# Image tiles kept as sums and differences of neighbours along the width, with filters rewritten for them, and the column levels of three batches moved to VectorE

## The chip, the cores and the metric

The kernel runs on one core of one Trainium2 chip. The metric is the device time of one execution in microseconds (us); lower is better. The engines are called as in the profile: PE (TensorE, matmuls), PEld (its weight loads), DVE (VectorE), ACT (ScalarE), POOL (GpSimd) and SP (SyncE, which here only issues DMAs).

## The reference

The input is x of shape (4, 64, 256, 256): 4 batches, 64 channels, images of 256 by 256, all in float32. Four layers follow each other.

```
layers 0, 1, 3:  y = conv2d(x, outer(hx, hy)) + x * bias      per channel, causal in both axes
                 hx, hy: 256 taps a channel, from a small sine network times a decay
layer 2:         f1 = haar2d(x)                               full 2-D Haar transform
                 acc = sum over i in (0, 1) of
                       shrink(einsum('bchw,oc->bohw', f1 * v[i], conv_w[i]), tau[i])
                 y = haar2d(acc, inverse=True) + x            shrink(f, t) = sign(f) * relu(|f| - t)
```

The filter of a convolution is an outer product, so a convolution is one causal product along the rows of the image and one along its width. A step of the Haar transform takes sums and differences of neighbours.

## The kernel before, in words

**A convolution.** For each batch b and channel c the image lies in SBUF as a tile of 128 partitions by 2 by 256, where row k * 128 + p is at partition p. `toeplitz` loads a tile `t` of 128 by 2 by 256 with one DMA from a padded filter in DRAM (`pads`): partition p gets the filter shifted by p, first the row filter, then the width filter. `contract` (L253, L254) multiplies the image as stationary operand with the filter read backwards. Since the filter is causal, the second half of the image meets only 128 columns. Each such product leaves the image transposed, so a product along the rows (`first`, to `pa`, copied to SBUF as `a` by ACT in L267) and one along the width (`second`, to `py`) bring it back. DVE adds bias times the input (`residual`, L284).

**Conv stage.** `convolutions` runs layers 0 and 1 for a batch: load `x`, `a0`, `y0`, `a1`, `y1`. Then `pairs` (L329, L330) takes sums and differences of neighbours along the width, the first level of the Haar transform. Both go to DRAM (`keep`). `levels` makes the further levels along the width, two of them on DVE and five on POOL, four channels at a time (L342, L343). `split` and `rest` (L361, L366) cut the result into two fp32r parts, `down` (L373, to `pz`) transforms along the columns with two matmuls, `away` stores to `coef`.

**Mixing stage.** `mixing` takes 64 groups of coefficients: `mix` is the matmul over channels (L441, to `px`), the scaling by v is shared by DVE (L460) and ACT (L465), then size and sign on ACT (L469, L472), and shrink, sign and sum on DVE (L476, L480, L486). The result collects in the resident tile `z`.

**Inverse stage.** `inverse` turns `z` back into images. The levels along the columns are done in place on `z` by DVE (`level`, `halve`: L291, L292), for chunks 1 to 3 of 16 channels each. For chunk 0, the first 16 channels, they are done by a matmul instead: after `rows` (L533, L534, to `pw`), `halves` (L540 on ACT, L541 on DVE) splits in two fp32r parts, and `cols` (L547, to `pu`) multiplies. `join` (L555, L558, L559) adds half of `keep` and spreads sums and differences back to neighbours, giving `u`. Then comes the convolution of layer 3 and the output, whose DMA ACT issues. Every third channel of batches 0 to 2 is put off: its `u` goes to DRAM (`late`), and its last convolution runs beside the mixing stage of batch 3 (`convolution`).

**Order.** Every step is entered with a time in ticks (a channel's or a group's turn) plus an offset from the table `PLACE`. The steps are sorted by that time and written out. The tile framework then orders each engine's instructions by their dependencies, and each engine works in its own order. Batch b+1's conv stage runs beside batch b's mixing stage; the inverse stage of b follows. `BUFS` and the `bufs` arguments give the number of buffers of a tag; a tile waits until the buffer used that many tiles ago is free. `toep` has 6.

## Time and profile before

| what | us |
|---|---|
| median of 3 runs | 2877.34 (2877.28 to 2879.65) |
| profiled execution, its own time | 2875.0 |
| its span, first to last instruction | 2873.2 |

In the span the stages lie as follows (first to last instruction of L441 and L533, rounded): conv of batch 0 alone to 446; mixing 0 to 868; inverse 0 to 1062; mixing 1 to 1523; inverse 1 to 1711; mixing 2 to 2172; inverse 2 to 2356; mixing 3 to 2641; inverse 3 to the end.

Rows of the page name the line, the engine, the operation, the tiles as out<-in, the shape and the count; then busy time in us, the mean of one in ns, and the idle time of the engine before them with what ended it. "128x256" is 128 partitions by 256 elements. One float32 matmul of the program is two instructions of the profile.

### The profile page before, as it was taken

How to read it: one execution, taken by the hardware profiler on the slowest of the kernel's cores; microseconds unless marked ns; L12 is line 12 of the kernel's file. 1: busy time of each engine (PE TensorE's matmuls, PEld its weight loads, DVE VectorE, ACT ScalarE, POOL GpSimd, SP SyncE). 2: the span in 40 equal slices, each digit the busy share in tenths (PEclk: the TensorE clock that was granted, in tenths of full speed). 3: DMA queues.
4: the chain of work that ended last, by engine and by line, in shares of the span. 5: the costliest groups of instructions: out<-in, count | busy, mean ns of one | idle time of the engine just before them, and what ended most of it. 6: DMA issues, size and time to landing. Idle time of an engine off the chain costs nothing. (4 is left out here: it accounts for less than half of the span.)

```text
span 2873.2 us, 52387 instructions
## 1 busy us (share of the span) xinstructions
PE 2819.8 (98%) x16566; PEld 2550.2 (89%) x16566; DVE 2498.0 (87%) x4263; ACT 2080.4 (72%) x4950; POOL 339.4 (12%) x644
## 2 busy tenths in 40 slices
PE   8999999999999999999999999999999999999999
PEld 6899998888888898998898998998888998888998
DVE  4655558999999779999999779999999779999985
ACT  2333338999995558998995658999995659998554
POOL 0111111121121001221221001221121000000000
PEclk9999999999999999999999999999999999999999
DMA  5877777666676986777777986777777988787786
GB/s 162 260 231 231 230 234 223 208 211 205 202 213 214 291 251 197 215 213 214 209 207 235 299 257 195 216 213 213 212 208 233 299 265 235 230 238 213 224 241 200
DMA packets 599367, 649.77 MB, mean 226 GB/s; under 512 B 48465, under 2 KB 517044, under 8 KB 598964
## 3 DMA queue, kind: packets, MB, share of 16 engines
q1 hardware_dynamic: 536996, 578.61, 68.2%
q10 hardware_dynamic: 62096, 67.82, 6.7%
q8 instruction: 134, 2.20, 0.3%
q14 instruction: 141, 1.16, 0.1%
HBM read 426.77 MB, written 219.48 MB: 225 GB/s over the span
## 5 line engine op out<-in xcount | busy, mean ns | idle before, releaser
L253 PE MATMUL py<-t,a 128*128 128x256 f32 x3072 | 922.2, 382 | 9.9 <-ACT a L267 9.2
L267 ACT COPY a<-pa 128x512 f32<-128x512 f32 x768 | 478.9, 624 | 495.5 <-PE pa L254 453.4
L465 ACT ACTIVATE f<-px,vt 128x64 f32<-128x64 f32 x2816 | 610.6, 367 | 101.4 <-DVE f L460 101.0
L254 PEld LDWEIGHTS py<-t,a 128*128 128x128 f32 x3072 | 583.4, 190 | 79.3
L254 PE MATMUL py<-t,a 128*128 128x128 f32 x3072 | 590.0, 274 | 0.0
L253 PEld LDWEIGHTS py<-t,a 128*128 128x128 f32 x3072 | 497.3, 191 | 51.1 <-ACT a L267 19.3
L441 PE MATMUL px<-wb,f 128*128 128x256 f32 x2048 | 487.6, 380 | 7.4 <-ACT f L465 7.3
L441 PEld LDWEIGHTS px<-wb,f 128*128 128x128 f32 x2048 | 369.0, 190 | 49.8 <-ACT f L465 10.2
L343 POOL TENSOR_TENSOR sd<-less 128x128 f32<-128x128 f32 (+4 forms) x320 | 192.7, 602 | 1855.5 <-DVE less L342 1537.6
L526 ACT COPY zc<-z 128x512 f32<-128x512 f32 x256 | 281.9, 1104 | 108.4 <-PE pw L534 99.6
L476 DVE TENSOR_TENSOR mag<-mag,vt 128x1024 f32<-128x1024 f32 x256 | 316.6, 1237 | 12.2 <-ACT mag L469 11.3
L480 DVE SCALAR_TENSOR_TENSOR mag<-mag,f 128x1024 f32<-128x1024 f32 x256 | 316.5, 1238 | 0.0
L253 PE MATMUL pa<-t,y 128*128 128x256 f32 x1024 | 308.9, 383 | 6.7 <-DVE y L284 5.2
L253 PE MATMUL pa<-t,x 128*128 128x256 f32 x1024 | 305.7, 380 | 0.0
L469 ACT ACTIVATE mag<-f 128x1024 f32<-128x1024 f32 x256 | 295.7, 1155 | 2.7 <-DVE z L486 0.4
L366 DVE TENSOR_TENSOR sp<-sd,sp 128x512 fp32r<-128x512 f32 x256 | 179.8, 702 | 127.8 <-ACT sp L361 126.7
L472 ACT ACTIVATE f<-f 128x1024 f32<-128x1024 f32 x256 | 285.8, 1116 | 3.5
L253 PE MATMUL pa<-t,u 128*128 128x256 f32 x772 | 232.1, 382 | 6.5 <-ACT w L540 2.8
L284 DVE SCALAR_TENSOR_TENSOR y<-x,bsb,py 128x512 f32<-128x512 f32 x256 | 190.7, 745 | 42.1 <-PE py L254 41.8
L254 PEld LDWEIGHTS pa<-t,y 128*128 128x128 f32 x1024 | 194.5, 190 | 26.3
L254 PEld LDWEIGHTS pa<-t,x 128*128 128x128 f32 x1024 | 194.6, 190 | 26.3
L284 DVE SCALAR_TENSOR_TENSOR y<-y,bsb,py 128x512 f32<-128x512 f32 x256 | 190.6, 745 | 27.7 <-PE py L254 27.3
(72 smaller groups left out, 4406.6 us busy)
## 6 DMA issues: line engine op xcount, KB each, us to landing
t<-pad SPq DMA_DIRECT2D x768, 256.0 KB, 4.1
x<-in_x SPq DMA_DIRECT2D x256, 256.0 KB, 3.8
coef<-co SPq DMA_DIRECT2D x256, 256.0 KB, 3.2
f<-coef SPq DMA_DIRECT2D x256, 256.0 KB, 3.1
r<-keep SPq DMA_DIRECT2D x256, 256.0 KB, 4.1
out_y<-y ACTq DMA_DIRECT2D x193, 256.0 KB, 4.2
keep<-sums SPq DMA_DIRECT2D x256, 128.0 KB, 2.9
keep<-sd SPq DMA_DIRECT2D x256, 128.0 KB, 2.8
```

Of the source, the lines that this page charges most:

```text
L253: nc.tensor.matmul(ps[:, m, :], src[:, 0, m * P : (m + 1) * P], t[:, ::-1], start=True, stop=False)
L254: nc.tensor.matmul(ps[:, m, P:], src[:, 1, m * P : (m + 1) * P], t[:, : P - 1 : -1], start=False, stop=True)
L267: nc.scalar.copy(a, s["p" + new])
L284: nc.vector.scalar_tensor_tensor(y, s[res], bsb[:, layer, c : c + 1], s["p" + new], ALU.mult, ALU.add)
L343: engine.tensor_tensor(t[:, :, :, half:length], v[..., 0], v[..., 1], ALU.subtract)
L441: nc.tensor.matmul(ps[:, q, h, :], f[:, q, h * P : (h + 1) * P], wb.rearrange("p r n -> p (r n)"), start=True, stop=True,)
L465: nc.scalar.mul(f4[:, j], px[:, j], scale(g, 0)[:, j : j + 1])
L469: nc.scalar.activation(mag, st[g]["f4"], AF.Abs)
L472: nc.scalar.activation(st[g]["f4"], st[g]["f4"], AF.Sign)
L476: nc.vector.tensor_sub(mag, mag, over(g, 1, 16))
L480: nc.vector.scalar_tensor_tensor(mag, mag, 0.0, st[g]["f4"], ALU.max, ALU.mult)
L526: nc.scalar.copy(a.rearrange("p h k i -> p (h k) i"), z[:, c // 16, :, :, c % 16].rearrange("p i x -> p x i"))
```

## The change

**Layout.** An image tile is now 128 by 4 by 2 by 64: for each half of the rows and each half of the width first 64 sums, then 64 differences of neighbours. The input and the output arrays are handed over with neighbours apart (even columns, then odd columns), one row of 2 KB a partition. POOL turns the input into sums and differences (`pairs`, now ahead of the convolutions) and turns the output back (`neighbours`; the very last one on DVE), two additions of 256 elements each. The sum of y1 writes straight to `sums` and `sd`, and `join` straight to `u`.

**Filters.** The row filter stays. The width filter is written in the basis of sums and differences: `filters` makes four runs of it (`runs`), and `toeplitz` fills the second half of `t` from these with two DMAs of 64 partitions; a third loads the first half. `along_width` reads this half of `t` as h, e, n with both h and n backwards, in runs of 64.

**Column levels.** In batches 0 to 2 chunk 0 takes the same way as the others, through `level`; `halves` and `cols` stay for batch 3 only. Where the levels stand has changed: for these batches more of them stand in the mixing stage, and the later ones are cut into pieces of 8, some with an order that keeps them behind the joins.

**Buffers.** Images, inputs, `u` and outputs share the tag "y", now with 9 buffers.

The diff, cut to its core:

```diff
-BUFS = {"res": 1, "y": 5, "co": 3}
+BUFS = {"y": 9, "co": 3}
 PLACE:
-    "load": 0.714,
+    "load": -1.0,
+    "pairs": 0.1,
+    "bands": 0.714,
-    "pairs": 4.639,
-    "out": 4.537,
+    "neighbours": 3.543,
+    "out": 5.2,
-    "l out": 4.4,
+    "l neighbours": 3.48,
+    "l out": 4.8,
 filters, end():
-            for axis, queue in enumerate((nc.scalar, nc.sync)):
-                queue.dma_start(pads[layer][:, axis, :], f[axis * C : (axis + 1) * C])
+            nc.sync.dma_start(pads[layer], f[:C])
+            g0, g1, g2 = (f[C:, i : i + S : 2] for i in range(3))
...
+            nc.vector.tensor_add(sums, g0, g2)
+            nc.vector.tensor_sub(less, g0, g2)
+            nc.vector.scalar_tensor_tensor(w[:, 0, 0, :P], sums, 0.5, g1, ALU.mult, ALU.add)
+            nc.vector.tensor_scalar(w[:, 0, 1, :P], less, -0.5, None, ALU.mult)
+            nc.vector.tensor_scalar(w[:, 1, 0, :P], less, 0.5, None, ALU.mult)
+            nc.vector.scalar_tensor_tensor(w[:, 1, 1, :P], sums, -0.5, g1, ALU.mult, ALU.add)
+            nc.scalar.dma_start(runs[layer], w)
 toeplitz:
-        nc.sync.dma_start(t, ap(pads[layer], c * 2 * ROW, [[1, P], [ROW, 2], [1, S]]))
+        nc.sync.dma_start(t[:, 0], ap(pads[layer], c * ROW, [[1, P], [1, S]]))
+        for i in range(2):
+            nc.sync.dma_start(
+                t[i * H : (i + 1) * H, 1].rearrange("p (o n) -> p o n", o=2),
+                ap(runs[layer], (c * 2 + i) * 2 * RUN, [[1, H], [RUN, 2], [1, P]]),
+            )
+    def along_width(ps, src, t):
+        t = t.rearrange("p (e h n) -> p h e n", e=2, h=2)[:, ::-1, :, ::-1]
+        v = ps.rearrange("p k (h e n) -> p k h e n", h=2, e=2)
+        for k in range(2):
+            for m in range(2):
+                nc.tensor.matmul(
+                    v[:, k, 1] if m else v[:, k],
+                    src[:, m, k * P : (k + 1) * P],
+                    t[:, 0] if m else t,
+                    start=(m == 0),
+                    stop=(m == 1),
+                )
+    def butterflies(engine, t, name):
+        new = io.tile([P, 4, 2, H], F32, name=name, tag="y", bufs=BUFS["y"])
+        engine.tensor_add(new[:, :, 0], t[:, :, 0], t[:, :, 1])
+        engine.tensor_sub(new[:, :, 1], t[:, :, 0], t[:, :, 1])
+        return new
 residual, for y1:
+                for e, to in enumerate((sums[:, c % 4], sd[:, c % 8, 1])):
...
+                    nc.vector.scalar_tensor_tensor(to, s[res][:, :, e], scale, ps[:, :, e], ALU.mult, ALU.add)
 pairs:
-            nc.vector.tensor_add(sums[:, c % 4], v[:, :, :, 0], v[:, :, :, 1])
-            nc.vector.tensor_sub(sd[:, c % 8, 1], v[:, :, :, 0], v[:, :, :, 1])
+            st[c]["x"] = butterflies(nc.gpsimd, st[c]["x"], f"xb_{b}_{c}")
 join:
-            nc.vector.scalar_tensor_tensor(t, st[c]["r"], 0.5, ps, ALU.mult, ALU.add)
...
-            nc.vector.tensor_add(v[:, :, :, 0], t[:, 0], t[:, 1])
-            nc.vector.tensor_sub(v[:, :, :, 1], t[:, 0], t[:, 1])
+            for e in range(2):
+                behind[0] = nc.vector.scalar_tensor_tensor(u[:, :, e], r[:, e], 0.5, w[:, e], ALU.mult, ALU.add)
 inverse:
+        if b + 1 < B:
+            for chunk in range(4):
+                for n in (1, 2, 4, 8):
+                    when(along + 12 + 3 * chunk, n, chunk)
+                when(along + 20 + 3 * chunk, 16, chunk)
+            for chunk in range(2):
+                for i in range(2):
+                    when(along + 37 + i + 3 * chunk, 32, chunk, 16 * i, 16)
+                for i in range(3 - chunk):
+                    when(along + 43 + 8 * i + 3 * chunk, 64, chunk, 16 * i, 16)
...
-            if c < 16:
+            if c < 16 and b + 1 == B:
                 at(start + c + PLACE["halves"], halves, c)
                 at(start + c + PLACE["cols"], cols, c)
 last:
+        def neighbours(c):
+            engine = nc.vector if b + 1 == B and c + 1 == C else nc.gpsimd
+            st[c]["y3"] = butterflies(engine, st[c]["y3"], f"out_{b}_{c}")
```

## The prediction

> **What bounds it now.** I read the page's busy times first, then busy times by stage, then the costliest groups, then single instructions where two engines compete.
>
> ```profile
> PE 2819.8 (98%) x16566; PEld 2550.2 (89%) x16566; DVE 2498.0 (87%) x4263; ACT 2080.4 (72%) x4950; POOL 339.4 (12%) x644
> ```
>
> PE is busy 98% of the span, and the granted clock is 1.00 in every stage. But 87% for DVE is a mean over unlike stages. Here the span is cut by stage: mixing and inverse of batch 0, of batch 1, then (after batch 2, like batch 1) of batch 3.
>
> ```profile
> 446.00:868.00 422.00, 416.30 (x2310) 371.58 (x2309) 414.07 (x696) 389.62 (x1109) 83.27 (x134) 1.00 0.69 208
> 868.00:1062.00 194.00, 185.17 (x1204) 168.70 (x1203) 162.72 (x294) 111.68 (x146) 7.21 (x17) 1.00 0.84 260
> 1062.00:1523.00 461.00, 458.83 (x2584) 413.50 (x2583) 449.11 (x743) 403.27 (x1127) 89.88 (x140) 1.00 0.71 208
> 1523.00:1711.00 188.00, 185.79 (x1218) 171.03 (x1217) 150.55 (x289) 113.11 (x148) 7.60 (x20) 1.00 0.86 274
> 2356.00:2641.00 285.00, 276.06 (x1497) 246.47 (x1497) 280.89 (x413) 268.37 (x702) 0.00 (x0) 1.00 0.78 230
> 2641.00:2863.00 222.00, 220.45 (x1447) 204.16 (x1446) 185.23 (x317) 115.34 (x145) 0.00 (x0) 1.00 0.75 226
> ```
>
> After the stage's length come the busy times of PE, PEld, DVE, ACT and POOL. In the mixing stages PE and DVE are both full (458.8 and 449.1 of 461). In the inverse stages PE alone is. In mixing 3 DVE is the fuller one (280.9 of 285), and POOL does nothing. So the time moves by what PE loses, by what PE waits for, and by what happens to DVE in mixing.
>
> **The change, part by part.**
>
> *Matmuls of the column levels.* L540, L541 and L547 go for 48 channels, 16 in each of three inverses.
>
> ```profile
> L547 PE MATMUL pu<-w,hb 128*128 128x512 f32 x128 | 46.4, 439 | 0.0
> L541 DVE TENSOR_TENSOR w<-pw,w 128x512 fp32r<-128x512 f32 x64 | 43.6, 686 | 0.2 <-ACT w L540 0.2
> L329 DVE TENSOR_TENSOR sums<-y 128x256 f32<-128x256 f32 x256 | 108.8, 425 | 2.7
> L330 DVE TENSOR_TENSOR sd<-y 128x256 f32<-128x256 f32 x256 | 108.6, 424 | 0.0
> L555 DVE SCALAR_TENSOR_TENSOR t<-r,pw 128x512 f32<-128x512 f32 x192 | 131.7, 686 | 67.5 <-PE pw L534 58.8 <-DMA r<-keep 5.0
> L558 DVE TENSOR_TENSOR u<-t 128x256 f32<-128x256 f32 x256 | 108.8, 425 | 6.3
> ```
>
> The busy time would price a pair at 46.4/64 = 0.725 us, but matmuls overlap. In the conv-only stage the like pair of L373 sits between an L254 issued at 300.14 and the next L253 at 300.83; without a pair that step takes 0.22 (301.26 to 301.48). So a pair costs 0.47, and 48 cost 22.6 (at most 34.8 by the busy time). All of it is on the full engine: **-22.6**.
>
> *Convolution matmuls.* The order of instructions of both kernels has the same 6144, with the same columns. New is that the filter of the width product is read in runs of 64 where it was one reversed run of 256. No row shows PE reading broken runs. Near rows are DVE's L329, which reads every second element (425 ns against 423 of the contiguous L187), and ACT's L385, which writes in regrouped runs (660 against 624 of L267). DVE's says nothing; ACT's 5.8% on 768 products of 1.30 us would be +58. I take 0, because only the addresses change, as in DVE's row; a gain is excluded, since no column goes.
>
> *DVE, convolutions.* L329 and L330 go (0.85 us a channel). The sum of y1 (745 ns for 512 elements) becomes two of 256: between 0.42 (the 256-element rows) and 0.49 (plus the 59 ns by which L284 exceeds L555), so 0.92 for two. A channel saves 0.67; the 59 channels inside mixing 1 save 40.
>
> *DVE, levels.* Chunk 0 adds 2 x (0.22+0.29+0.42+0.69+1.23+2.45+4.90) = 20 us a batch at the rows of L291/L292. But the scheduler of before already pulled levels into mixing 1. Counting the program orders between first scaling and last add, level work there goes from 46 to 42 us, in mixing 0 from 32 to 42. Together DVE loses 44 us in mixing 1 and 2, and 53 x 0.67 - 10 = 26 in mixing 0; mixing 3 stays as it was.
>
> *DVE, inverses.* A join is two operations of 256 instead of 686 + 425 + 424 ns: 0.67 less for 64 channels, and 11 us of L541 go. PE's idle time there is 8.8, 2.2 and 2.8 us in inverses 0 to 2, most of it at the first channels, where the removed route and the levels queue on DVE. I take 8 of 13.8 back, and 3 of the 8.9 around mixing 3's end and the 1.6 of inverse 3: **-11**. In mixing 1 and 2, where DVE was as full as PE, PE gives up its 2.2 us of idle each and about as much in delayed issues: **-8**, between 0 and -10.
>
> *POOL.* New are 1022 additions of 256 elements: two for each input in conv (128 in each of mixing 0 to 2), two for each output (126 in mixing 3, 86 in an inverse). In the conv-only stage POOL takes 292 ns for 64 and 393 for 128 elements, so 0.6 us for 256, 1.2 a channel of 5.7 to 7 us: no bound by itself. The price is on DVE, and the rows show it:
>
> ```profile
> L342 POOL TENSOR_TENSOR less<-less 128x128 f32<-128x128 f32 x17 | 6.7, 393 | 0.0
> ```
>
> ```profile
> L342 POOL TENSOR_TENSOR less<-less 128x128 f32<-128x128 f32 x14 | 10.8, 775 | 1.8 <-DVE sd L343 1.8
> ```
>
> ```profile
> 1250.34 0.62 DVE L343 TENSOR_TENSOR sd<-less 128x256 f32<-128x256 f32 x1
> 1250.88 1.21 DVE L480 SCALAR_TENSOR_TENSOR mag<-mag,f 128x1024 f32<-128x1024 f32 x1
> 1252.02 1.42 DVE L476 TENSOR_TENSOR mag<-mag,vt 128x1024 f32<-128x1024 f32 x1
> 1253.36 0.73 DVE L284 SCALAR_TENSOR_TENSOR y<-x,bsb,py 128x512 f32<-128x512 f32 x1
> ```
>
> ```profile
> 1251.04 2.55 POOL L342 TENSOR_TENSOR less<-less 128x128 f32<-128x128 f32 x2 [0.36 <-DVE sd L343]
> 1253.54 0.29 POOL L343 TENSOR_TENSOR sd<-less 128x64 f32<-128x64 f32 x1
> ```
>
> The first row is POOL's in the conv-only stage, the second the same operation in mixing 1: 393 against 775 ns. Then one piece of mixing 1: two POOL operations of 0.69 together last 2.55 while DVE runs operations with two inputs in SBUF, and DVE's L476 (mean 1.23) takes 1.42, its L343 0.62 for 0.43. Once DVE runs the sum that reads PSUM, POOL goes at full speed. So one such cluster (ten POOL operations, 496 elements) cost DVE 0.38 us, or 0.20 scaled to 256 elements; the rise of DVE's means over the stage comes to some 0.21 a cluster, or 0.11. I take **0.15 an addition**, with 0 and 0.6 as ends: 19 us a mixing stage. In mixing 0 to 2 that is less than the 26 and 44 that DVE loses: 0. In mixing 3 nothing covers it: 19 less DVE's slack of 4, **+15** (-0 to +72).
>
> The Trainium skill, page "SBUF — State Buffer", section "Who interferes with whom", says that a DVE instruction with two SBUF inputs and a GpSimd instruction that reads SBUF exclude each other for the whole instruction. Taken at its hardest, each addition would hold DVE for its whole 0.6 us, which is the upper end above; the rows show POOL doing most of the waiting.
>
> *DMA and SP.* A filter tile comes in three DMAs, not one: 1536 more issues at 0.36 to 0.44 us, 1.6 us a channel in conv. SP waits 169 of 300 us between 100 and 400, and the additions take 85 of it. Bytes stay; rows of 512 B against 1 KB for half the filter, 2 KB against 1 KB for inputs and outputs. Each DMA waits for the one eight issues before it: ten a channel, all at today's slowest landing there (4.3 us), need 5.4 of the 5.67 us. 0, with little margin. ACT's output DMA now waits for POOL, 1.66 ticks (4.8 us) after it could start: 0.
>
> *Ends.* Six small operations behind each filter (1.5 us) lie under the warming matmuls: +1 (0 to 3). The last output gets two additions on DVE: **+0.9**.
>
> Sum: -22.6 - 11 - 8 + 15 + 1 + 0.9 = -24.7. The profiled execution took 2875.0 (span 2873.2 and 1.8 around it), the median 2877.3. So 2850 against the profiled one, 2852 as a median.
>
> **Rivals.**
> *Contention on DVE decides (slower).* With d us lost per addition, mixing 3 loses 126d - 4, mixing 0 128d - 26, mixing 1 and 2 128d - 44 each. The other terms give -39.7; from d = 0.28 on the change is a loss. At 0.43 (a 256-element operation of DVE's length) it is 50+29+11+11-40 = +61, 2938; at 0.6 about +148, 3025. For it: DVE is full in mixing, two thirds of its time has two SBUF inputs. Against: 0.11 to 0.20 measured. Chance 0.18.
> *PE reads broken runs slower.* +58 on the forecast, 2910. Chance 0.04.
> *SP or the eight in flight become the bound in conv.* From 4.6 us a landing on; at 5.0 the tick is 6.25, 64 x 0.58 = +37 in the conv-only stage alone, 2889. Chance 0.05.
> *The work leaves PE, but the joints hide it:* waits at stage borders stay and mixing 3 takes the rest, 2872 to 2883 or just under. Chance 0.09.
> *No contention and all waits go:* -22.6 - 25 - 10 + 2 = -56, 2821. Chance 0.09.
>
> **Numbers.** Forecast 2852, 0.55 (d from 0 to 0.26, 2833 to 2871). A measurement here tells 0.2% (5.8 us). Faster: 0.55, the last rival's 0.09 and half of the hidden case, 0.68. Same: the rest of that case and 0.05 of contention and SP near their deciding points, 0.10. Slower: 0.22. The range 2815 to 2895 takes in d up to 0.34 and SP's price, and leaves out the hard contention and broken runs.
>
> **What would show it.** L547's successor with 32 instead of 128 matmuls; PE about 2790 busy; DVE near 2180 and what POOL costs it, POOL at 1000 to 1700 with means far over 0.6 us in mixing; mixing 1 within 10 us of its length, mixing 3 longer by 10 to 20, inverses 0 to 2 shorter by 8 to 18. Wrong if DVE's 1024-element means in mixing rise by over 0.1 us, if PE's 256-column step leaves 0.22 us, or if PE waits for filter DMAs.

## The result, and the profile after

The changed kernel takes 3072.9 us (median of 4 runs, 3068.1 to 3080.4) against 2877.3 us of the kernel before: 1.0678 times as long, with an interval of 1.0665 to 1.0692. It is slower by 196 us where 25 us less was forecast. The profiled execution took 3072.6 us, its span 3070.8. The busy times of the whole span, from the page of the changed kernel:

```profile
PE 2873.0 (94%) x16470; PEld 2547.3 (83%) x16470; DVE 2417.7 (79%) x3882; ACT 2053.5 (67%) x4902; POOL 1304.9 (42%) x1666
```

PE was busy 98% of the span before and is 94% now; DVE 87% and 79%. POOL went from 339 to 1305 us. No engine but POOL is fuller than it was, and yet the span is 198 us longer: the time went into waiting. The stages show where. From here on the span is cut by one rule, the matmuls to `px`: "conv" runs to the first of a batch, "mixing" from its first to its last, "inverse" on to the next batch's first. (The prediction's cut gave the mixing stages of before some 14 to 26 us more and the inverses as much less.) The columns are those of the prediction's table; the rows are inverse 0, mixing 1, mixing 3 and inverse 3 of the changed kernel.

```profile
909.00:1135.00 226.00, 208.39 (x1298) 185.35 (x1297) 147.22 (x276) 115.93 (x158) 87.21 (x118) 0.99 0.82 243
1135.00:1596.00 461.00, 440.38 (x2430) 390.81 (x2429) 429.85 (x656) 387.25 (x1095) 219.22 (x250) 1.00 0.71 198
2509.00:2820.00 311.00, 278.55 (x1432) 236.29 (x1431) 305.49 (x387) 257.75 (x677) 136.36 (x115) 0.99 0.73 205
2820.00:3071.00 251.00, 239.40 (x1546) 220.87 (x1545) 169.34 (x284) 126.82 (x172) 121.62 (x142) 0.99 0.77 214
```

Mixing 1 and mixing 3 of the kernel before, by the same cut:

```profile
1063.00:1497.00 434.00, 431.83 (x2423) 388.89 (x2422) 422.42 (x704) 385.42 (x1091) 85.34 (x131) 1.00 0.71 208
2356.00:2627.00 271.00, 264.70 (x1433) 236.56 (x1433) 267.13 (x392) 257.60 (x677) 0.00 (x0) 1.00 0.79 232
```

In mixing 1 PE now has 20.6 us of idle time where it had 2.2, in mixing 3 32 where it had 6. The granted clock is 0.99 to 1.00 in these rows and 0.996 over the span, against 1.000 before; 0.4% of 3071 us is some 12 us (an estimate), so it is not the main cause. The lengths of all stages, of every run that computes them, in us (one execution each; the four of the changed kernel lie within 12 us):

| kernel | one run | conv | mixing 0, 1, 2, 3 | inverse 0, 1, 2, 3 |
|---|---|---|---|---|
| before | 2875.0 | 446.9 | 398.6, 434.7, 434.7, 271.1 | 217.2, 213.5, 210.5, 245.9 |
| changed | 3072.6 | 492.3 | 416.9, 460.5, 461.1, 311.2 | 226.3, 226.7, 225.1, 250.7 |
| a1 one filter DMA | 3016.6 | 451.0 | 418.5, 458.7, 457.7, 312.5 | 220.6, 225.9, 221.2, 248.8 |
| a2 no input additions | 2996.2 | 487.5 | 396.1, 434.2, 434.3, 313.4 | 222.4, 230.1, 225.7, 250.8 |
| a3 no output additions | 2980.1 | 492.3 | 418.2, 459.1, 459.6, 273.2 | 206.1, 214.7, 211.4, 243.6 |
| a4 none of the three | 2835.3 | 449.5 | 394.9, 434.4, 434.4, 271.1 | 200.0, 204.2, 201.4, 243.3 |
| b1 before, levels on DVE | 2890.1 | 448.8 | 401.4, 434.0, 433.9, 271.1 | 221.0, 217.1, 214.7, 246.0 |
| b2 the same, behind the joins | 2893.0 | 447.6 | 412.7, 434.1, 434.1, 271.2 | 214.1, 217.3, 214.2, 245.9 |
| d1 output additions of inverses on DVE | 3037.7 | 488.3 | 415.5, 459.5, 459.7, 312.8 | 214.1, 220.9, 216.1, 248.9 |
| d2 output DMA a tick later | 3077.2 | 493.9 | 420.5, 460.3, 459.4, 311.3 | 222.8, 229.9, 226.9, 250.3 |
| e1 before, three filter DMAs | 2911.3 | 467.3 | 398.7, 434.9, 435.0, 271.1 | 223.3, 218.5, 215.1, 245.6 |
| e2 all additions on DVE | 3007.5 | 488.6 | 427.9, 441.4, 439.7, 305.0 | 215.8, 219.4, 215.2, 252.7 |
| e3 halves cut by output | 3831.0 | 686.3 | 481.6, 538.5, 547.1, 317.2 | 306.8, 316.3, 310.5, 325.0 |
| f1 run DMAs of batch 0 from ACT | 3037.9 | 462.9 | 415.6, 462.2, 460.3, 311.0 | 221.8, 227.6, 225.7, 248.8 |
| f3 each addition where it is cheapest | 2975.1 | 465.4 | 415.1, 440.4, 439.9, 312.0 | 215.4, 221.8, 214.8, 248.5 |

Every stage lost. Two places in the trace show how. First, SP in the conv stage, the changed kernel's DMA issues over one channel's turn (start, length, queue, line):

```profile
300.03 0.33 SPq L396 DMA_DIRECT2D keep<-sums  x1
300.51 0.33 SPq L397 DMA_DIRECT2D keep<-sd  x1
300.93 0.46 SPq L386 DMA_DIRECT2D x<-in_x  x1
301.48 0.41 SPq L260 DMA_DIRECT2D t<-pad  x1
301.94 1.24 SPq L262 DMA_DIRECT2D t<-run  x2
303.27 0.54 SPq L260 DMA_DIRECT2D t<-pad  x1
303.91 0.38 SPq L449 DMA_DIRECT2D coef<-co  x1
304.34 1.25 SPq L262 DMA_DIRECT2D t<-run  x2
```

One issue follows the other with some 0.1 us between; the next turn's first starts at 305.69. SP hardly waits for anybody here, and PE waits for filter tiles: 17.6 us between 100 and 400 us, against 0.8 before. Before, the same turn held six issues of 0.33 to 0.38 us and over half of it lay between them. That SP bounds this stage is what f1 tests below.

Second, DVE in mixing 1 of the changed kernel (groups with their shapes; count, busy us, mean ns, idle before):

```profile
L544 DVE SCALAR_TENSOR_TENSOR mag<-mag,f 128x1024 f32<-128x1024 f32 x62 | 84.3, 1359 | 1.0
L540 DVE TENSOR_TENSOR mag<-mag,vt 128x1024 f32<-128x1024 f32 x62 | 82.2, 1326 | 8.9 <-ACT mag L533 8.7
L550 DVE TENSOR_TENSOR z<-mag 128x256 f32<-128x256 f32 x124 | 61.5, 525 | 0.4
L341 DVE SCALAR_TENSOR_TENSOR y<-xb,bsb,py 128x512 f32<-128x512 f32 x56 | 41.3, 737 | 0.0
...
L524 DVE TENSOR_TENSOR f<-px,vt 128x256 f32<-128x256 f32 x63 | 26.1, 414 | 0.0
```

The first two in the same stage of before:

```profile
L480 DVE SCALAR_TENSOR_TENSOR mag<-mag,f 128x1024 f32<-128x1024 f32 x62 | 76.1, 1227 | 0.0
L476 DVE TENSOR_TENSOR mag<-mag,vt 128x1024 f32<-128x1024 f32 x62 | 76.2, 1229 | 3.0 <-ACT mag L469 2.7
```

The other three took 428, 746 and 423 ns there. Those with both inputs in SBUF (L544, L540, L550) became 0.10 to 0.13 us longer; those that read one input from PSUM, the memory in which PE's products land (L341, L524), did not. POOL's additions, 0.68 us alone, take 1.05 and 1.31 us in this stage. PE, and ACT, wait for DVE:

```profile
PE pa L276 <- DVE y L341: 19.5, 21, 2.0
```

```profile
ACT f L529 <- DVE f L524: 67.1, 50, 3.0
```

(Total, times, longest; from the waits of PE and of ACT in mixing 1.) The first was 1.3 us before, the second 39.0; in a4, the changed kernel without its additions and extra filter DMAs (below), they are 0.9 and 42.1.

### The profile page after: what moved, and what is told of

Same layout as the page of the kernel before. It is cut to its first block, busy times and chain, and to the rows that moved or that the text cites. A ratio compares the mean times of both kernels' runs of the same rounds, so it can differ in the third digit from the quotient of the medians.

```text
span 3070.8 us, 55140 instructions
## 1 busy us (share of the span) xinstructions
PE 2873.0 (94%) x16470; PEld 2547.3 (83%) x16470; DVE 2417.7 (79%) x3882; ACT 2053.5 (67%) x4902; POOL 1304.9 (42%) x1666
## 5 line engine op out<-in xcount | busy, mean ns | idle before, releaser
L290 PE MATMUL py<-t,a 128*128 128x256 f32 (+1 forms) x6144 | 1148.5, 330 | 60.5 <-ACT a L316 59.9
L290 PEld LDWEIGHTS py<-t,a 128*128 128x128 f32 x6144 | 1016.1, 191 | 206.4 <-ACT a L316 97.0
L316 ACT COPY a<-pa 128x512 f32<-128x512 f32 x768 | 477.6, 622 | 598.5 <-PE pa L276 442.2
L301 POOL TENSOR_TENSOR xb<-x 128x256 f32<-128x256 f32 x256 | 249.6, 975 | 780.7 <-DMA x<-in_x 696.6
L301 POOL TENSOR_TENSOR out<-y 128x256 f32<-128x256 f32 x255 | 219.4, 860 | 676.9 <-DVE y L341 586.7
L276 PE MATMUL pa<-t,y 128*128 128x256 f32 (+1 forms) x2048 | 391.9, 335 | 69.4 <-DVE y L341 53.2
L276 PEld LDWEIGHTS pa<-t,y 128*128 128x128 f32 x2048 | 330.9, 191 | 124.3 <-DVE y L341 76.4
L276 PE MATMUL pa<-t,xb 128*128 128x256 f32 (+1 forms) x2048 | 378.7, 328 | 8.5 <-DMA t<-pad 4.5
L590 ACT COPY zc<-z 128x512 f32<-128x512 f32 x256 | 277.0, 1097 | 135.0 <-PE pw L598 54.9
L276 PEld LDWEIGHTS pa<-t,xb 128*128 128x128 f32 x2048 | 331.6, 191 | 39.2 <-issue 6.8
L540 DVE TENSOR_TENSOR mag<-mag,vt 128x1024 f32<-128x1024 f32 x256 | 339.9, 1328 | 23.2 <-ACT mag L533 22.4
L544 DVE SCALAR_TENSOR_TENSOR mag<-mag,f 128x1024 f32<-128x1024 f32 x256 | 339.1, 1324 | 2.2
L341 DVE SCALAR_TENSOR_TENSOR y<-u,bsb,py 128x512 f32<-128x512 f32 x193 | 143.9, 745 | 245.7 <-issue 135.2
L276 PE MATMUL pa<-t,u 128*128 128x256 f32 (+1 forms) x1544 | 286.9, 329 | 6.0 <-PE pw L598 6.0
L302 POOL TENSOR_TENSOR xb<-x 128x256 f32<-128x256 f32 x256 | 286.2, 1118 | 0.0
```

The source lines that it names most:

```text
L276: nc.tensor.matmul(ps[:, m, k * P :], src[:, k, m], t[:, : k * P - 1 if k else None : -1], start=(k == 0), stop=(k == 1),)
L290: nc.tensor.matmul(v[:, k, 1] if m else v[:, k], src[:, m, k * P : (k + 1) * P], t[:, 0] if m else t, start=(m == 0), stop=(m == 1),)
L301: engine.tensor_add(new[:, :, 0], t[:, :, 0], t[:, :, 1])
L302: engine.tensor_sub(new[:, :, 1], t[:, :, 0], t[:, :, 1])
L316: nc.scalar.copy(a, s["p" + new])
L540: nc.vector.tensor_sub(mag, mag, over(g, 1, 16))
```

## The experiments

Three theories stood for the loss. **Lock:** POOL's additions keep DVE from its operations with two SBUF inputs. **Queue:** three DMAs a filter tile are too many for SP. **Order:** ACT stands at the output's DMA, which now waits for POOL, and everything behind it in ACT's order is late (the trace shows ACT's copy L316 waiting 81 us for the output's additions). A fourth was the prediction's own rival, that PE reads broken runs slower.

**a1, one DMA a filter tile.** The layout, the additions and PE's broken runs stay; the tile comes in one DMA from the padded filter as before, so the second half holds the filter in the plain basis.

```diff
-        nc.sync.dma_start(t[:, 0], ap(pads[layer], c * ROW, [[1, P], [1, S]]))
-        for i in range(2):
-            nc.sync.dma_start(t[i * H : (i + 1) * H, 1]...., ap(runs[layer], ...))
+        nc.sync.dma_start(t, ap(pads[layer], c * 2 * ROW, [[1, P], [ROW, 2], [1, S]]))
```

> The changed kernel, but each filter tile comes in one DMA of 128 partitions as before (the width filter is then the plain one, not the one in sums and differences; the six operations that make it are left out too). Queue theory (the three issues a tile fill SP's queue): the conv-only stage, which the change made 45 us longer (446.9 to 492.3 at the first matmul of L505), goes back to within 5 us of 447, inverses 0 to 2 (9 to 14 us longer each) give back 5 to 15 us each; in all 2990 to 3015. Lock theory (POOL's additions hold DVE): these stages keep their lengths, mixing keeps 417, 460, 460 and 311; 3060 or more.

3016.6 us: 56 us come back, 41 of them in the conv stage (492.3 to 451.0), some 12 in the inverses, nearly none in mixing. PE still reads broken runs of 64, and the conv stage is 4 us from that of before.

**a2, no additions of the inputs.**

```diff
-            st[c]["x"] = butterflies(nc.gpsimd, st[c]["x"], f"xb_{b}_{c}")
+            pass
```

> The changed kernel without POOL's additions on the inputs (the input is used as it is loaded, neighbours apart but not added). Lock theory: mixing 0 to 2, which the change made 18, 26 and 26 us longer, lose 15 to 30 us each, mixing 3 keeps its 311; 2990 to 3010. Queue theory: at most 5 us in all, 3065 to 3075. The conv-only stage keeps its 492 in both.

2996.2 us: 76 us come back, 74 of them in mixing 0 to 2 (20.8, 26.3, 26.8).

**a3, no additions of the outputs**, and the output's DMA at its old place.

```diff
-            st[c]["y3"] = butterflies(engine, st[c]["y3"], f"out_{b}_{c}")
+            pass
```

> The changed kernel without the additions on the outputs (sums and differences are stored as they are; the output DMA is issued at the times of the kernel before). Lock theory: mixing 3 goes from 311 back to 270 to 280 us. Order theory (ACT's queue stands still at an output DMA that waits for POOL, and the copies behind it feed PE): inverses 0 to 3 lose 10 to 20 us each. Both: 2970 to 3010. Queue theory alone: 3065.

2980.1 us: 92 us come back, 38 in mixing 3 and 53 in the four inverses.

**a4, all three left out.**

> All three of the above together: one DMA a filter tile, no additions on inputs and outputs. What is left of the change is the removed matmuls, the shorter joins and sums on DVE, the moved levels, the runs of 64 in which PE reads the filter. If additions and queue explain the loss, 2820 to 2850, as the forecast had it without contention; if something else in the change costs time (the reading in runs, the placing of the levels), above 2877.

2835.3 us, 42 less than before. The three single gains add up to 225, together they give 237: the losses are nearly separate. What is left is the rest of the change, and it brings in total what the prediction had put on it. Mixing 1 of this kernel:

```profile
1044.00:1478.00 434.00, 432.28 (x2425) 388.94 (x2425) 394.48 (x653) 384.91 (x1092) 81.50 (x132) 1.00 0.71 209
```

DVE is down from 422 to 394 us of busy time, PE is busy 432 of 434 as it was, and the stage is as long as before: PE bounds it, and DVE's relief of 28 us gave it nothing.

**b1, the column levels alone**, in the layout of before: chunk 0 of batches 0 to 2 goes through `level` as in the change.

```diff
+        if b + 1 < B:
+            for n in (1, 2, 4, 8):
+                when(along + 12, n, 0)
...
-            if c < 16:
+            if c < 16 and b + 1 == B:
```

> The kernel before with one part of the change alone: in batches 0 to 2 chunk 0's column levels go through DVE (no split, no matmuls of L547 for these 48 channels), placed in the mixing stage where the change has them. Layout, filters, additions and output stay as before. The PE term of the prediction expects -22.6 us, and the run without additions gave inverses 9 to 17 us shorter; DVE gets 20 us of levels a batch and loses 11 of the split. If PE's 22.6 us come back and DVE, full in mixing, can take the levels: 2850 to 2860. If the levels find DVE full, mixing 0 to 2 grow by up to 9 us each and it ends at 2865 to 2880.

2893.4 us over 4 runs, 1.0053 of before (1.0036 to 1.0070). Each of the first three inverses has 7.5 us less of matmuls (by the prediction's price) and is 4 us longer. PE's `pw` waits 18.5 us in all for DVE's join, a wait that the trace of before does not have; it had 2.9 us for the removed split (L541) in its place.

**c1, the lock by itself.** A program that computes nothing of the reference: DVE alone, POOL alone, both at once.

```python
wide:   nc.vector.tensor_add(r[:, i % 4], a[:, 0], a[:, 1])                      # 1024 elements
narrow: nc.vector.tensor_sub(r[:, i % 4, :256], a[:, 0, :256], a[:, 1, :256])
single: nc.vector.tensor_mul(r[:, i % 4, :512], a[:, 0, :512], ps)               # one input in PSUM
adds:   nc.gpsimd.tensor_add(w[:, i % 4, :size], g[:, 0, :size], g[:, 1, :size]) # 256 or 64
```

> Not the computation of the reference: a program of separate parts, an all-engine barrier between them, to measure the disputed costs alone. (1) 24 DVE additions of 1024 elements, both inputs in SBUF; (2) 24 POOL additions of 256; (3) both together; (4) POOL's beside 64 DVE subtractions of 256; (5) POOL's beside 48 DVE products of 512 with one input in PSUM; (6) 48 POOL additions of 64 beside DVE's of 1024; then 12 DMAs each: 128x2x256, 128x256, 64x2x128, 128x2x128, 64x256. Lock theory: (3) lasts as long as both sums (27 + 17 = 44 us; DVE's mean grows by 0.5 or more), (4) the same, (5) as the longer alone (29 us). Lenient contention as in the prediction (0.15 us an addition): (3) 31 us. Queue theory: the issue of 64x2x128 takes 0.55 to 0.6 us against 0.35 to 0.4; whether by the 64 partitions or by the two runs shows in the other two.

DVE's side (start, length, engine, count):

```profile
13.13 27.34 DVE L50 TENSOR_TENSOR r<-a 128x1024 f32<-128x1024 f32 x24 [3.13 <-SPq L46]
57.18 39.45 DVE L50 TENSOR_TENSOR r<-a 128x1024 f32<-128x1024 f32 x24 [16.71 <-SPq L46]
97.37 34.20 DVE L54 TENSOR_TENSOR r<-a 128x256 f32<-128x256 f32 x64 [0.73 <-SPq L46]
131.69 28.79 DVE L58 TENSOR_TENSOR r<-a,ps 128x512 f32<-128x512 f32 x48
160.60 30.19 DVE L50 TENSOR_TENSOR r<-a 128x1024 f32<-128x1024 f32 x24
```

and POOL's 24 additions by themselves:

```profile
40.67 16.36 POOL L62 TENSOR_TENSOR w<-g 128x256 f32<-128x256 f32 x24 [38.52 <-SPq L46]
```

With both inputs in SBUF, alone, DVE's 24 operations of 1024 take 27.34. Beside 24 additions of 256 elements (second line) they take 39.45: 12.11/24 = **0.50 us an addition**. Beside 48 additions of 64 elements (last line) they take 30.19: 2.85/48 = **0.06 us** an addition (0.07, if only the 39 that fit beside it are counted: POOL's 48 took 36.97). Beside 64 subtractions of 256 (third line) it is 0.52: DVE's operations start every 0.86 us while POOL runs and every 0.33 after. With one input in PSUM (fourth line) POOL's 24 additions beside it took 16.48, as alone, and DVE's operations started every 0.60 us with POOL and without. So the price is not in proportion to the elements. POOL's addition of 256 takes 0.68 alone and costs DVE 0.50; one of 64 took 0.29 in the conv stage of before and costs 0.06. Both cost what they last less some 0.2 us. The lock theory's 44 us for the second line, the sum of both, was not reached. The same program's DMA part, twelve of each form on SP: the change's form, 64 partitions by two runs, takes 0.57 to 0.65 us to issue, 64 partitions by one run of 1 KB 0.45 to 0.60, 128 partitions by two runs 0.36 to 0.47. The longer issue goes with the 64 partitions more than with the two runs.

**d1, the outputs' additions of the inverses on DVE**, where POOL's were; those in mixing 3 stay on POOL.

```diff
-            engine = nc.vector if b + 1 == B and c + 1 == C else nc.gpsimd
+            engine = nc.gpsimd if queue is nc.sync else nc.vector
```

> The changed kernel, but in the inverse stages the additions on the outputs run on DVE (0.82 us a channel, DVE is busy 150 of 226 us there); the late channels' beside mixing 3 stay on POOL. Order and lock theories both expect inverses 0 to 2 at 208 to 217 us instead of 225 to 227, as without these additions (206 to 215): 3030 to 3045. If the added DVE work itself delays PE's chain, 225 or more stay: 3065 to 3080. Mixing 3 keeps its 311.

3037.7 us, 35 less: the inverses are 12, 6, 9 and 2 us shorter although DVE's busy time in inverse 0 rises from 147 to 168 us. The lock and the order theory both expect that.

**d2, the output's DMA one tick later**, so that ACT doesn't stand at it.

```diff
-    "out": 5.2,
+    "out": 6.2,
```

> The changed kernel with the output DMA issued one tick later (offset 6.2 instead of 5.2), the additions staying on POOL. Order theory: ACT no longer stands at an output DMA that waits for POOL (now 81 us before its copies and 23 before its fetches), so inverses 0 to 3 fall by 8 to 15 us each: 3030 to 3045. Lock theory: POOL still holds DVE, inverses within 4 us of now: 3062 to 3075.

3077.2 us, no gain. But the edit hardly took away the wait that it was meant for: ACT's copies still wait 76 us for the output's additions, and its fetches (L590) 14 where they waited 23. So the run doesn't decide about the order theory. In inverse 0 of the changed kernel DVE's busy time is only 6 us above a3's (147.2 against 141.1), ACT waits 10.5 us for POOL's output additions, PE waits 10.8 us for ACT's `a` (3.7 in a3), and the stage is 20 us longer. How much of the inverses' loss is the lock and how much ACT's order stays open.

**e1, the queue by itself:** the kernel before with three filter DMAs.

```diff
-        nc.sync.dma_start(t, ap(pads[layer], c * 2 * ROW, [[1, P], [ROW, 2], [1, S]]))
+        nc.sync.dma_start(t[:, 0], ap(pads[layer], c * 2 * ROW, [[1, P], [1, S]]))
+        for i in range(2):
+            nc.sync.dma_start(t[i * 64 : (i + 1) * 64, 1]..., ap(pads[layer], ... + i * 64, [[1, 64], [P, 2], [1, P]]))
```

> The kernel before, with nothing of the change except that a channel's filter tile is loaded by three DMAs, as in the changed kernel: one of 128 partitions x 256 elements and two of 64 partitions x 2 runs of 128. The values are the ones of before; no addition is moved, no basis changed. If the DMA issues on SP are a price of their own, the conv-only stage goes from 446.9 to about 488 to 492 us, as in the changed kernel, the inverses grow by 2 to 6 us each, the mixing stages stay within 2 us, and the time is 2920 to 2940. If the conv-only stage of the changed kernel is long because the additions on POOL come between the input's DMA and the first product, it stays at 447 and the time at 2877 to 2885.

2911.3 us. The conv stage grew by 20, not by 41 to 45; the inverses by 6, 5 and 5, mixing not at all. The number was a miss. One difference: the two runs lie side by side in DRAM here, and such a DMA's issue has a median of 0.48 us, against 0.59 in the changed kernel. How SP's time divides between 120 and 420 us, by channel (from the issues in the trace; a tick is the mean time from one store to `coef` to the next, a gap the time from one issue's end to the next one's start):

| kernel | tick, us | DMAs on SP | issuing | gaps under 0.3 | gaps over 0.3 |
|---|---|---|---|---|---|
| before | 5.67 | 6.1 | 2.38 | 0.50 | 2.78 |
| a1 | 5.71 | 6.1 | 2.43 | 0.43 | 2.84 |
| e1 | 6.09 | 10.2 | 5.18 | 0.79 | 0.13 |
| changed | 6.45 | 10.2 | 5.60 | 0.76 | 0.08 |
| e3 | 9.15 | 10.0 | 8.19 | 0.77 | 0.19 |
| f1 | 5.83 | 6.4 | 2.69 | 0.40 | 2.75 |

In e1, the changed kernel and e3 there is no room left: the tick is what SP's issues take.

**e2, all additions on DVE**, none on POOL.

```diff
-            st[c]["x"] = butterflies(nc.gpsimd, st[c]["x"], f"xb_{b}_{c}")
+            st[c]["x"] = butterflies(nc.vector, st[c]["x"], f"xb_{b}_{c}")
-            engine = nc.vector if b + 1 == B and c + 1 == C else nc.gpsimd
+            engine = nc.vector
```

> The changed kernel with every sum and difference of an input or an output (1022 instructions) on DVE, none on POOL; POOL keeps what it did before the change. If the additions cost through the lock between POOL and DVE (0.3 to 0.5 us each in DVE's time), then DVE doing them itself at 0.42 costs about the same: mixing 0 to 2 within 10 us of the changed kernel's 417, 460 and 461, mixing 3 310 to 325, the inverses 5 to 12 us shorter as in the run with the output's additions on DVE, the time 3010 to 3060. If instead POOL's own latency (an addition of 0.9 to 1.1 us there) delays the products, then without it mixing 0 to 2 return to 397 to 440 and the time is below 2990. The conv-only stage stays at 485 to 492 by both, since the filter's DMAs stay.

3007.5 us, between the two. Mixing 1 and 2 are 19 and 21 us shorter than with POOL, mixing 0 is 11 longer, mixing 3 6 shorter. The stage that tells most is mixing 1 of this run:

```profile
1132.00:1573.00 441.00, 434.76 (x2426) 390.21 (x2425) 426.15 (x765) 385.23 (x1092) 77.36 (x130) 1.00 0.74 206
```

DVE is nearly as busy here (426.2) as in the changed kernel's mixing 1 (429.9), and yet the stage takes 441 and not 461. PE waits 1.4 us for DVE's `y` here (19.5 there), ACT 37.3 for `f` (67.1). The lock's cost isn't only the time by which DVE's rows grow.

**e3, the halves cut by output** instead of by partitions: the same count of DMAs and bytes.

```diff
-        for i in range(2):
-            nc.sync.dma_start(t[i * H : (i + 1) * H, 1]..., ap(..., [[1, H], [RUN, 2], [1, P]]))
+        for o in range(2):
+            nc.sync.dma_start(t[:, 1, o * P : (o + 1) * P], ap(..., [[2 * RUN, 2], [1, H], [1, P]]))
```

> The changed kernel with the filter's second half loaded by two DMAs as well, but cut by output columns instead of by partitions: each fills 128 partitions x 128 elements where each filled 64 partitions x 2 runs of 128. The count of DMAs, the bytes and the values are the same. If the price is the longer issue of a DMA into 64 partitions (0.59 us against 0.38 for 128 partitions), 4 of 10 issues a channel get 0.2 us shorter, 0.8 us a channel, and the conv-only stage falls from 492 to 447 to 460 us, the time to 3020 to 3040. If the price is the count of DMAs (ten a channel with eight in flight), the stage stays at 485 to 495 and the time at 3060 to 3080.

3831.0 us (granted clock 0.953): both theories missed by far. The issues themselves are shorter when they go through (median 0.51), but many of SP's issues, of nearly all kinds, stand 1 to 2.5 us, and the tick has 8.19 us of issuing.

**f1, the run DMAs of the first batch from ACT's queue.**

```diff
-    def toeplitz(layer, c, name):
+    def toeplitz(layer, c, name, queue=nc.sync):
...
+            toeplitz(0, c, f"t0_{b}_{c}", nc.sync if b else nc.scalar)
```

> The changed kernel with the two 64-partition DMAs of every filter tile of the first batch issued by ACT instead of SP (four a channel); SP keeps the other six. In the conv-only stage of the changed kernel a tick of 6.45 us is 5.60 of SP's issues, 0.76 between them and 0.08 of waiting. If SP's issuing is the bound, SP falls to about 3.4 us a tick, ACT (22% busy there) has room for 4 issues of 0.6, and the stage falls from 492 to 448 to 460 us, the time to 3030 to 3045. If the DMA queues behind SP are the bound (the landing, or the eight in flight), the stage stays above 475.

3037.9 us: 35 less, 29 of it in the conv stage (492.3 to 462.9, 3 above the range expected). The transfers are the same; only who issues them changed. That takes them out of SP's queue too, but the DMAs in flight were not the bound: in the changed kernel SP's issues between 120 and 420 us start 1.6 us (median) after the landing of the DMA eight issues before, and only 8 of the 296 whose landing the trace gives within 0.2 us of it. So it is SP's issuing. The 12 us by which this stage is still longer than a1's 451.0 are not explained.

**f2, the DMA forms by themselves**, 24 of each from SP.

```python
L66: nc.sync.dma_start(t[:, i], ap(pads, ..., [[1, P], [S + P, 2], [1, S]]))           # whole tile, 256 KB
L70: nc.sync.dma_start(t[h * H : (h + 1) * H, ...], ap(runs, ..., [[1, H], [RUN, 2], [1, P]]))   # the change's, 64 KB
L77: nc.sync.dma_start(t[:, ..., o * P : (o + 1) * P], ap(runs, ..., [[2 * RUN, 2], [1, H], [1, P]]))  # e3's, 64 KB
L82: nc.sync.dma_start(t[:, i, 0, :P], ap(pads, ..., [[1, P], [1, P]]))                # plain, 64 KB
```

> A measurement program alone, nothing of the reference is computed. DMAs into a filter tile, one form after the other, each form by itself, first from SP's queue and then from ACT's: 128 partitions x 2 runs of 256; 64 partitions x 2 runs of 128; 128 partitions x one run of 128 read as two groups of 64 partitions; 128 partitions x one plain run of 128. If the issue's time goes with the form, the second takes 0.57 to 0.62 us and the first and the last 0.32 to 0.47; the third tells why the kernel with halves cut by output columns was slower (3831 us): either its issue is long (over 0.6) or its transfers are (steps far above those of the second).

```profile
23.84 15.62 SPq L66 DMA_DIRECT2D t<-pad  x24
45.18 15.62 SPq L70 DMA_DIRECT2D t<-run  x24
63.12 34.60 SPq L77 DMA_DIRECT2D t<-run  x24
102.36 11.26 SPq L82 DMA_DIRECT2D t<-pad  x24
```

24 DMAs of a quarter tile in the change's form take SP as long (15.62 us) as 24 of the whole tile. One issue is 0.61 us nearly throughout, against 0.36 to 0.47 for most of the whole-tile ones and 0.43 for the plain form. e3's form settles at some 1.45 us each after the first three (0.60, 0.51, 0.81), with nothing else running. From ACT's queue the four take 15.64, 15.81, 35.09 and 11.46.

The Trainium skill, page "DMA: Bandwidth & Descriptors", section "Why a DMA increments its semaphore by 16 and not by 1", says that a DMA is spread over the largest number of engines up to 16 that divides the slowest dimension of both its patterns. The slowest dimension of e3's source is 2. That would put each of its DMAs on two engines. The trace agrees: while SP issues the change's form (first row) and e3's (second), the mean busy share of the 16 DMA engines, the number before the last, is 0.42 and 0.14, and 0.14 of 16 is 2.2 engines.

```profile
46.00:61.00 15.00, 0.00 (x0) 0.00 (x0) 1.00 0.42 96
65.00:97.00 32.00, 0.00 (x0) 0.00 (x0) 1.00 0.14 43
```

**b2, the levels alone with the change's order:** b1 with the later levels in pieces of 8, each behind the join issued last.

```diff
+        if stay and behind[0] is not None:
+            tc.add_manual_dep(first.ins, behind[0].ins.name, order, reason="not ahead of the joins")
```

> The kernel before in its own layout, with the first three batches' column levels all on VectorE (192 us of it as there are in the changed kernel) and with the changed kernel's order: levels in the inverses in pieces of 8 blocks, each held behind the join issued last. The run with the levels alone, without that order, took 1.0053 of before, with the inverses 4 us longer although PE has 7.5 us less in each. If the joins' queue behind the levels was the cause, the inverses fall to 205 to 212 us from 217, 213 and 210, and the time is 2850 to 2872. If DVE simply has no room for the levels in this layout, the inverses stay at 214 to 221 and the time is 2880 to 2895.

2890.2 us over 5 runs, 1.0036 of before (1.0022 to 1.0051). (All levels of three batches are 12 chunks of 20.4, some 245 us, not the 192 of the expectation.) Inverse 0 falls by 3 us, inverses 1 and 2 grow by 4, and mixing 0 pays 14 for the levels moved into it. That is what the second theory expected, that this layout has no room on DVE for them; other places for the levels were not tried.

**f3, each addition where it was cheapest:** f1, with inputs on POOL for batches 0 and 1 and on DVE for 2 and 3, outputs as in d1.

> The changed kernel with each addition where the runs found it cheapest, and the first batch's 64-partition DMAs on ACT's queue: inputs' additions on POOL for batches 0 and 1 and on DVE for batches 2 and 3, outputs' additions on DVE in the inverses and on POOL in mixing 3. If the losses are separate, they add up: about -40 in the conv-only stage, -20 in each of mixing 1 and 2, -30 in the inverses, 2955 to 2975 us. If a common cause lies behind them, the time stays above 3000. Below 2877 by neither.

2975.1 us, at the upper edge of the sum of the separate gains, and still 98 above before. No run here that makes the additions beats the kernel before; a4, which is 42 faster, makes none.

## Why the prediction was wrong, point by point

The sum had four parts; the runs give each its own size. The four add up to 182 us of the 196; the rest shows only with all of them together, and is hardly more than the 12 us by which the changed kernel's own runs differ.

| part | forecast, us | measured, us | by |
|---|---|---|---|
| everything but additions and filter DMAs | -39.7 | -42 | a4 against before |
| three DMAs a filter tile (with the six operations that make the runs) | 0 | +56 | changed against a1 |
| additions of inputs | 0 | +76 | changed against a2 |
| additions of outputs | +15 | +92 | changed against a3 |

- **Right: the work that leaves PE, and the inverses' waits.** -22.6 and -11 were put on the inverses; in a4 they are 17, 9, 9 and 3 us shorter, 38 in all.
- **Right: broken runs cost PE nothing.** With them the conv stage of a1 is 451.0, and the eight instructions of a product along the width step in 1.31 us in the changed kernel (301.96 to 303.27), as in the product along the rows.
- **Wrong, though small: -8 in mixing 1 and 2 from DVE's relief.** In a4 DVE is busy 28 us less there (44 were forecast) and the stage is 434.4 against 434.7. The lengths of DVE's operations fall by some 40 us, but the operations overlap: in c1 those of 256 elements last 0.42 and start every 0.33 us. PE's idle time there was only 2 us; the "as much again in delayed issues" did not show. The head and tail (+1.9) can't be told apart from the 2.6 by which a4's conv stage is longer.
- **The step that failed first: "0.15 us an addition".** It took ten small POOL operations of 496 elements in all, which cost DVE 0.38, and scaled by elements to 256. The price isn't proportional: c1 gives 0.06 for 64 elements and 0.50 for 256, that is, each instruction's own time less some 0.2. The smaller of the ten last 0.20 to 0.23 us alone (in the conv stage of before), so by this rule nearly all of the 0.38 came from the few larger ones. In mixing 3 of the changed kernel DVE's busy time grew by 38.6 over a4's nearly equal stretch (266.9 to 305.5), for 115 POOL additions 0.34 each; the stage is 40 us longer than a4's. In mixing 1 it is 35.4 for 113, 0.31 each. c1's 0.50 times the prediction's own two thirds, the share of DVE's time with two inputs in SBUF, gives 0.33 (an estimate). The rival priced at 0.43 an addition, given 0.18, was the nearest in mixing 3: it said 50, and 40 was measured. The price alone did not decide, though: with 0.34 the prediction's own sum gives 2894, still inside its range (39 in mixing 3, 18 in mixing 0, nothing in mixing 1 and 2). The next three steps hold the rest.
- **The second: the cover.** In mixing 0 to 2 the price was held against the 26 and 44 us that DVE loses, and booked as 0. In mixing 1 DVE lost 28, not 44. The additions made its busy time grow by 35 over a4's (394.5 to 429.9), less than the 40 us of room that a4 leaves it, and the stage grew by 26 all the same. Room that is there on the mean did not cover the stalls here: from a4 to the changed kernel ACT's wait for DVE's `f` grows from 42 to 67 us, DVE's for ACT's `sp` from 7.8 to 15.8, PE's for DVE's `y` from 0.9 to 19.5. (DVE's wait for `mag`, 2.7 before and 8.7 after, is 8.9 in a4 already and so not the additions'.) In e2, with nearly the same busy time on DVE but the additions in its own order, the stage loses only 7. That it is a stall in whichever operation is running that hurts more than work queued at a place of its own is how I read this pair; no run isolates it.
- **The third: the inverses.** The output additions there (86 in each of the first three, 126 in the last) had no term of the sum at all; DVE has some 31 us idle there before (194 less 162.7 in inverse 0). They cost 53 us in four inverses (a3). The busy time that DVE loses there is too small for it (6 of 20 us in inverse 0); whether the rest is the lock's stalls or ACT standing at the output's DMA, which the prediction also put at 0, no run separates.
- **The fourth: SP.** "1536 more issues at 0.36 to 0.44 us" took the price of a 128-partition DMA for one of 64 partitions with two runs of 512 bytes; it has 0.59 in the changed kernel (median) and 0.61 alone, and a full SP lengthens the others too (t<-pad 0.51 us on the mean in this stage, 0.41 before over the run). A tick of SP's work became 5.60 + 0.76, not 2.4 + 1.6 + 0.8 = 4.8. The rival for SP asked for landings over 4.6 us; between 100 and 400 us they are 3.4 for `run` and 3.8 for `pad`, shorter than the 4.3 of before. The bound came from the issuing, which the rival did not price. Two of the prediction's own signs of being wrong came true: one of DVE's 1024-element means in mixing rose by 0.13 us (over 0.1 was the sign), and PE waited for filter DMAs.
- **Two readings in its numbers.** Its 0.55 case, "d from 0 to 0.26, 2833 to 2871", is counted from two bases (2877.3 and 2875.0), and its lower end takes mixing 3's slack of 4 for a gain; from the median it is 2838 to 2874. That changes nothing in the outcome.
- **What the skill said of these steps.** The Trainium skill, page "SBUF — State Buffer", section "Who interferes with whom", has DVE operations with two SBUF inputs and POOL's reads exclude each other for the whole instruction. The prediction weighed this and set it aside for the row of small operations. c1 bears it out for the most part (0.50 of 0.68), and also the page's statement that a DVE operation with one input in SBUF doesn't contend. Page "DMA: Bandwidth & Descriptors", section "Rules for kernel authors", advises against two transfers to disjoint partition halves, and for one of 128 partitions. It gives another reason, that the transfers serialize; here it was the issue, 2 x 0.61 us where one whole tile takes 0.36 to 0.47.

## What to carry to other kernels

Do not scale a contention price by elements from small operations: measure one at the size that will run (here 0.50 us alone and 0.31 to 0.34 in the kernel), and do not hide it behind the mean room of an engine that two others wait for. Price a new DMA by the nearest issue of the same partitions and runs, and add up the issuing queue over one turn, gaps included, before calling it free. When several parts of a change could each have lost the time, leave them out one by one and then all together: here that gave the size of each and showed that the rest of the change works. And look into the trace whether an edit took away the wait that it was meant for, before a theory is dropped: in d2 it did not.

## What the runs showed that was not expected

- An issue into 64 partitions with two runs (64 KB) takes 0.61 us on SP and 0.62 on ACT, longer than most issues of a whole tile of 256 KB (0.36 to 0.47).
- e3's DMAs, whose source has an outermost dimension of 2, took 1.45 us each in a row with 2.2 of 16 DMA engines busy, and the kernel with 1536 of them 3831 us.
- POOL's additions cost DVE 0.06 us at 64 elements and 0.50 at 256.
- Work taken off PE made the kernel slower where DVE had to take it over (b1 and b2, +0.5% and +0.4%): PE was 98% busy, but in the inverses it then waits for DVE's joins (`t`, 18.5 and 11.2 us).
